# A perceiver layer on one core: the first 512 context rows by seven half-size products, their keys turned through DRAM

## The chip, the cores and the metric

The kernel runs on one core of a Trainium2 chip. A core has TensorE (PE, matrix products, with PEld its weight loads), VectorE (DVE), ScalarE (ACT), GpSimd (POOL) and SyncE (SP, which here only issues DMAs). Each engine works through its own queue in order. The metric is the device time of one execution, in microseconds (us), as the median of three executions.

## The reference

One layer with three parts on 256 tokens `x` of width 512: cross attention, a state-space block, and a mixture of 32 experts. Only the first part matters here:

```
xn = layernorm(x)                              # 256 x 512
q, k0, v0 = xn @ wq, xn @ wk, xn @ wv          # 16 heads, 4 key heads, head size 128; q and k0 are
                                               # normed per head and rotated by position (rope)
k1, v1 = ctx @ wk_ctx, ctx @ wv_ctx            # ctx: 4096 x 512; each product is 4096 x 512; keys normed
out = softmax(q [k0 k1]^T) [v0 v1]             # the 256 own keys are masked causally
x = x + out @ wo
```

Everything is float32.

## The kernel before

The context's 4096 rows are cut into eight steps of 512 rows (`NC = 8`, `CK = 512`). The attention goes through stage s = 0, the 256 own tokens, and then s = 1 to 8, one context step each. While stage s runs its scores (L668) and values (L693), the keys and values of the next context step are computed beside it, so step 0 is computed before the attention, in an opening stage, together with the own keys, queries and values.

**The two ways of a context step.** A step multiplies a 512 x 512 block of `ctx` with `[wk_ctx | wv_ctx]`, 512 x 1024. Steps 1 to 7 use `fast_steps`, a recursive scheme of seven products (a Strassen form: sums and differences of the quarters of both operands, seven products in place of eight), on two levels. Step 0 is done plainly by `context_pieces(0)`: for each of four tiles of 128 rows, `key_piece` and `value_piece` make a 128 x 512 result from four matmuls each (L225, helper `project`), ACT copies it out of PSUM, `key_rms` squares the keys on ACT and makes a factor on POOL, and `key_transpose` (L296 to L302) turns the four heads of a tile by four PE transposes and an ACT copy. In the profile a float32 matmul with 512 columns shows as two records, so a piece is eight records.

**Turning without PE.** `turn_heads` (L264 to L273) turns a 128 x 512 tile otherwise: DVE transposes 32 x 32 blocks into a tile `tr`, SP issues four stores of `tr` to a DRAM block (`kd` or `qd`), and then one load of the turned block into `kT` or `qT`, which waits until the stores have landed. These five DMAs are pinned in program order on SP's queue. `tr` has two buffers. Own keys and the queries of heads 0 to 11 are turned so (eight blocks of 128 x 512: k0, k1, q00, q01, q10, q11, q20, q21; q with the group of four heads first, then the token tile). The queries of the last group are turned by PE (`selfT`, L575).

**One own block** (`self_block`): four matmuls into one of two PSUM banks of `ps_mm`; ACT copies the bank to `raw` (tag `kraw`, two buffers) and squares it; DVE makes the rope in four instructions (L541 to L544, `norm_rope`) into `o`, one of five rooms; POOL makes the norm (L200) and multiplies `o` by it (L545); then `turn_heads`.

**Order.** A planner puts the instructions of each engine in one fixed order before the kernel runs, by program order and by when it reckons inputs and buffers to be free. `tc.issue_after(ins)` queues what a block issues on the engine of `ins` behind `ins`; `tc.keep_in_program_order` pins an instruction behind all earlier ones of its engine. The list at L603 to L618 writes the opening stage out by hand: context values, own keys, the last context key tile, queries, own values, and the preparation of the weights for `fast_steps` (`weights_of`, `one`, `two`).

**Weight sums.** `weight_sums` (POOL, L338 to L340) makes the three 256 x 512 combinations T1, T2, T4 of the weights' quarters; `last_sum` (L387 to L390) makes T3 in place (`b12 = b22 - b12`, DVE) and the second-level sums of the value weights (`second_sums("wv")`, POOL, four instructions of L379 to L382) during stage 0, behind a mask of the attention.

**Loads.** SP loads, in this order: context tile 0 of step 0, `wk_ctx` quarters 0 and 1, then 2 and 3 in one, `x`, context tile 1, tiles 2 and 3, `wv_ctx`, then `wk`, `wq` group 0, `wv`, `wq` groups 1 to 3, and context steps 1 and 2 into the two buffers of `ctxp`.

Of the kernel before, what the change touches and what calls it, by code (L numbers as in the profile page):

```python
# [19 lines left out]
P = 128  # L20
# [55 lines left out]
def perceiver_layer(ctx: ExitStack, tc: tile.TileContext, a: dict, out: bass.AP):  # L76
# [25 lines left out]
    load_wkc(2, 2)  # L102
    nc.sync.dma_start(x_sb, a["x"].rearrange("(t p) d -> p t d", p=P))
    load_ctx0(1, 1)
    load_ctx0(2, 2)
    nc.sync.dma_start(wvc, a["wv_ctx"].rearrange("(k p) n -> p k n", p=P))
# [34 lines left out]
    def layer(ctx, bounded):  # L141
# [71 lines left out]
        def turn_xn(t, tp, halves=False):  # L213
# [4 lines left out]
            for copy, ks in (((V.tensor_copy, slice(0, KD // 2)), (S.copy, slice(KD // 2, KD))) if halves else  # L218
                             ((V.tensor_copy, slice(0, KD)),)):
                copy(xT[:, ks, t * P:(t + 1) * P], tp.rearrange("p (k n) -> p k n", k=KD)[:, ks])  # L220
# [22 lines left out]
        ctx_tiles = {0: ctx0}  # L243

        def load_ctx(c):
            ct = ctxp.tile([P, CK // P, KD, P], FP, tag="ctx", name="ctx")
            nc.sync.dma_start(ct, a["ctxT"][c])
            ctx_tiles[c] = ct

        wk = wpiece(a["wk"], "wk")  # L250
        wq = [wpiece(a["wq"][:, 0:512], "wq0")]
        wv = wpiece(a["wv"], "wv")
        wq += [wpiece(a["wq"][:, j * 512:(j + 1) * 512], f"wq{j}") for j in range(1, 4)]
        load_ctx(1)
# [55 lines left out]
        def context_pieces(c):  # L310

            ct = ctx_tiles.pop(c)
            v, r, raws, key_transpose, _ = context_tiles(c)

            def key_piece(i):
                ps = ps_mm.tile([P, 512], FP, tag="mm", name="ps_k")
                project(ps, lambda k: ct[:, i, k, :], lambda k: wkc[:, k, :])
                raws[i] = raw = krp.tile([P, NKV, HD], FP, tag="kraw" if i == 1 else "kn", name="kraw")
                S.copy(raw, ps.rearrange("p (h d) -> p h d", d=HD))
                key_rms(raw, r[:, i, :])  # L320

            def value_piece(i):
                ps = ps_mm.tile([P, 512], FP, tag="mm", name="ps_v")
                project(ps, lambda k: ct[:, i, k, :], lambda k: wvc[:, k, :])
                S.copy(v[:, i, :], ps)

            return [[lambda i=i, f=f: f(i) for i in range(CK // P)] for f in (key_piece, value_piece, key_transpose)]

# [55 lines left out]
        def last_sum():  # L387

            V.tensor_tensor(b12, b22, b12, ALU.subtract)
            each(second_sums("wv"))  # L390
# [3 lines left out]
        def fast_steps(c, behind=None):  # L394
# [19 lines left out]
            def sums():  # L414
# [4 lines left out]
                left("P6", S2)  # L419
                G.tensor_tensor(S3, a11, a21, ALU.subtract)  # L420
# [110 lines left out]
        heads_done = []  # L531

        def norm_rope(ps, t, tb):
# [10 lines left out]
            V.tensor_tensor(o, o, u, ALU.add)  # L544
# [7 lines left out]
        ctx_k, ctx_v, ctx_t = context_pieces(0)  # L552
        for t in range(NT):
            normed = layernorm(t)
        for i in range(3):
            ctx_k[i]()
        for t in range(NT):
            turn_xn(t, ps_sc.tile([P, 512], FP, tag="sc", name="lnT"))
        rope_table(tab_k, kw_bc)
        rope_table(tab_q, qw_bc)  # L560
# [27 lines left out]
        turns = ctx_t[0:3]  # L588

        def last_key():  # L590
            ctx_k[3]()
            return ctx_t[3]
# [8 lines left out]

        weights_of = lambda: next(placed)
        one, two = lambda: behind_head("t"), lambda: behind_head("t4", 2)  # L603
        for f in (ctx_v[0], lambda: k_of(0), lambda: k_of(1), last_key, *q[0], ctx_v[1], weights_of, lambda: self_value(0),
                  q[1][0], one, q[1][1], one, lambda: self_value(1), weights_of, q[2][0], one, q[2][1], one, ctx_v[2],
                  q[3][0], two, q[3][1], two, ctx_v[3]):
            turn = f()
            if f not in (weights_of, one, two):
                turns.append(turn)
            while len(turns) > 2:  # L610
# [23 lines left out]
        pin(nc.sync.dma_start(by_head, a["by_head"].partition_broadcast(P)))  # L634
# [1180 lines left out]
```

## Time and profile before

| | us |
|---|---|
| median of 3 executions | 963.77 (963.64 to 963.96) |
| the profiled execution | 961.0 |
| its span (first to last instruction) | 959.2 |
| PE busy in the span | 939.9 |
| DVE, ACT, POOL busy | 571.4, 383.0, 429.3 |
| opening stage, from the first matmul to the last plain piece | 5.45 to 78.9 |
| stage 0 of the attention | 79.3 to 101.1 |

The span is one profiled execution, and the profile's times count from its start. A group line gives the source line, engine, operation, output and inputs, shape, number, the time busy and the mean of one; a timeline line gives start, time, the same names, and in brackets how long the engine sat idle before it and what ended that. PE's busy time is modelled, since matmuls are pipelined, so the distances between starts are the better measure of what one costs.

### The profile page before, as it was taken

To read this page: it belongs to the slowest core of one execution; us is meant where nothing else is said; L and a number is where in the kernel's file an instruction comes from. 1 tells how busy PE (TensorE), PEld (TensorE's weight loads), DVE (VectorE), ACT (ScalarE), POOL (GpSimd) and SP (SyncE) were. 2 spreads that over 40 slices of the span, in tenths; PEclk is the share of its full clock that TensorE was granted. 3 is DMA by queue.
4 is the path that set the end of the run, shared out by engine and by line. 5 is a ranking of instruction groups with operands and counts; after the bars stand their busy time and mean duration, and the time that the engine had idled before them with its cause. 6 is when DMAs were issued, how large, how long until landed. Compare 5 with 4: busy or idle time off the path is not lost.

```text
span 959.2 us, 10117 instructions
## 1 busy us (share of the span) xinstructions
PE 939.9 (98%) x3025; PEld 508.0 (53%) x3025; DVE 571.4 (60%) x1205; ACT 383.0 (40%) x872; POOL 429.3 (45%) x487
## 2 busy tenths in 40 slices
PE   7999999999999999999999999999999999999996
PEld 3444555555555555555555555544465655555442
DVE  4458766566566656665756656658497666632223
ACT  3646444344344444343443444443253742122221
POOL 3559956345444644634724723300013234545542
PEclk9999999999999999999999999999999999999999
DMA  9732053053034015104205203360046453899983
GB/s 328 241 78 47 0 176 87 1 154 89 1 86 141 15 35 174 35 14 152 77 1 153 67 1 88 81 228 0 0 157 209 165 196 122 327 328 366 362 322 109
DMA packets 130803, 124.93 MB, mean 130 GB/s; under 512 B 80017, under 2 KB 99250, under 8 KB 125490
## 3 DMA queue, kind: packets, MB, share of 16 engines
q1 hardware_dynamic: 119216, 77.96, 26.9%
q0 software_dynamic: 7904, 40.90, 11.7%
q10 hardware_dynamic: 3618, 5.33, 1.5%
q8 instruction: 26, 0.43, 0.2%
q14 instruction: 39, 0.32, 0.1%
HBM read 88.76 MB, written 35.41 MB: 129 GB/s over the span
## 4 chain that ended last, share of the span: by engine, by line
PE 95%; issue 1%; POOL 1%; DVE 1%; DMA 1%; ACT 0%; SPq 0%; POOLq 0%; DVEq 0%
PE oT L693 24%; PE scT L668 24%; PE ps_kv L459 15%; PE ps_egu L225 5%; PE ps_self L225 4%; PE ps_v L225 2%; PE ps_o L892 2%; PE ps_xbc L225 2%; PE ps_k L225 2%; PE ps_ye L1616 2%; PE ps_out L1089 1%; PE ps_z L225 1%; PE ps_sgu L225 1%; PE ps_ye L1619 1%; PE xgTp L1495 1%
## 5 line engine op out<-in xcount | busy, mean ns | idle before, releaser
L684 DVE TENSOR_TENSOR lacc<-lacc,prT 128x512 f32<-128x512 f32 x256 | 200.6, 785 | 197.3 <-ACT prT L674 196.2
L674 ACT ACTIVATE prT<-scT,bq,rk 128x512 f32<-128x512 f32 x256 | 198.4, 775 | 280.4 <-PE scT L668 269.5
L668 PE MATMUL scT<-qT,kT 128*128 128x512 f32 x536 | 273.5, 592 | 0.0
L693 PE MATMUL oT<-prT,v 128*128 128x512 f32 x528 | 269.4, 592 | 0.1
L693 PEld LDWEIGHTS oT<-prT,v 128*128 128x128 f32 x528 | 100.1, 190 | 125.8 <-issue 117.9
L668 PEld LDWEIGHTS scT<-qT,kT 128*128 128x128 f32 x536 | 101.2, 190 | 41.0 <-issue 30.6
L459 PE MATMUL ps_kv<-fast,ctx 128*128 128x256 f32 x350 | 99.6, 379 | 0.0
L459 PEld LDWEIGHTS ps_kv<-fast,ctx 128*128 128x128 f32 x350 | 66.4, 190 | 48.3 <-issue 39.9
L410 POOL TENSOR_TENSOR ctx<-ctx 128x128 f32<-128x128 f32 x21 | 11.4, 542 | 98.7 <-PE ps_kv L459 98.7
L200 POOL TENSOR_TENSOR rk<-pv,mhalf 128x4 f32<-128x4 f32 x32 | 37.4, 1180 | 28.0 <-DVE pv L199 28.0
L262 ACT ACTIVATE xn<-kraw 128x128 f32<-128x128 f32 x112 | 33.5, 301 | 39.4 <-POOL kraw L434 22.1
L459 PE MATMUL ps_kv<-wkv,ctx 128*128 128x256 f32 x168 | 48.9, 379 | 0.0
L444 POOL TENSOR_TENSOR v<-fast,v 128x768 f32<-128x768 f32 x21 | 40.9, 1960 | 16.2 <-DVE fast L488 15.6
L459 PEld LDWEIGHTS ps_kv<-wkv,ctx 128*128 128x128 f32 x168 | 31.8, 190 | 28.4 <-issue 25.0
L699 DVE TENSOR_TENSOR oacc<-oT,oacc 128x512 f32<-128x512 f32 x64 | 43.6, 682 | 0.0
L1599 DVE TENSOR_TENSOR hid<-si,ps_egu 128x128 f32<-128x128 f32 x18 | 5.2, 287 | 47.5 <-ACT si L1597 47.5
L459 PE MATMUL ps_kv<-fast,fast 128*128 128x256 f32 x112 | 33.3, 379 | 0.0
L459 PEld LDWEIGHTS ps_kv<-fast,fast 128*128 128x128 f32 x112 | 21.3, 190 | 17.8 <-issue 12.0
L268 DVE STREAM_TRANSPOSE tr<-kraw 128x512 f32<-128x512 f32 x28 | 18.3, 690 | 19.6 <-POOL kraw L433 19.6
L892 PE MATMUL ps_o<-wo,qT 128*128 128x512 f32 x64 | 28.8, 592 | 0.0
L1290 POOL DMA_INDIRECT xg_sb<-xg,place x16 | 15.1, 947 | 29.1 <-PE xgTp L1495 26.7
L225 PE MATMUL ps_self<-wq,xT 128*128 128x512 f32 x64 | 28.1, 592 | 0.0
(439 smaller groups left out, 1412.8 us busy)
## 6 DMA issues: line engine op xcount, KB each, us to landing
xg<-xn SPq DMA_DIRECT2D x6, 2560.0 KB, 9.4
ctx<-in_ctxT_dram SPq DMA_DIRECT2D x7, 1024.0 KB, 5.0
kd<-tr SPq DMA_DIRECT2D x112, 64.0 KB, 2.2
kT<-kd SPq DMA_DIRECT2D x28, 256.0 KB, 3.0
ye<-y_sb ACTq DMA_DIRECT2D x19, 256.0 KB, 8.3
wq<-in_wq_dram SPq DMA_DIRECT2D x4, 1024.0 KB, 14.4
wo<-in_wo_dram SPq DMA_DIRECT2D x4, 1024.0 KB, 7.9
w_in<-in_W_inT_dram SPq DMA_DIRECT2D x4, 1024.0 KB, 8.7
```

The costliest lines, as they stand in the source:

```text
L200: return G.tensor_tensor(dst, v[:, :n], mhalf[:, :n], ALU.pow)
L225: TE.matmul(ps, lhs(k), rhs_of(k), start=(k == 0), stop=(k == KD - 1))
L262: S.activation(sq[:, h, :], raw[:, h, :], AF.Square, accum_out=ss[:, h:h + 1])
L444: G.tensor_tensor(to[:, 1:4], q, base[:, 1:4], ALU.add)
L459: TE.matmul(b[n], sets[name][i], y, start=start, stop=True, skip_group_check=True)
L668: scored.append(TE.matmul(sc, kT[:, g, i * P:(i + 1) * P], qT[:, t, heads4(g), :].rearrange("p h q -> p (h q)"), start=True, stop=True).ins)
L674: S.activation(pr, sc, AF.Exp, bias=shift, scale=SCALE if r is None else r[:, i, g:g + 1])
L684: V.tensor_tensor(la, la, pr, ALU.add)
L693: TE.matmul(outs[g, t], v[:, i, g * HD:(g + 1) * HD], pr, start=(n == 0), stop=last)
L699: V.tensor_tensor(ov, outs.pop((g, t)), ov, ALU.add)
L892: TE.matmul(m["ps_o", t], aT[:, t, h, :], wo[j][:, h % 4, :], start=(h == 0), stop=(h == NH - 1))
L1616: TE.matmul(ps[i], h[:, i, :], wd[i], start=True, stop=False)
```

## The change

Step 0 is computed by seven products on one level (`first_step`). With A the four quarters of the context block (a11, a12, a21, a22: two row tiles by two halves of the inner dimension) and B those of `[wk_ctx | wv_ctx]` (b11, b21 the key weights, b12, b22 the value weights):

```
S1 = a21 + a22;  S2 = S1 - a11;  S3 = a11 - a21;  S4 = a12 - S2      (POOL)
T1 = b12 - b11;  T2 = b22 - T1;  T3 = b22 - b12;  T4 = b21 - T2
P1 = a11 b11   P2 = a12 b21   P3 = S4 b22   P4 = a22 T4   P5 = S1 T1   P6 = S2 T2   P7 = S3 T3
keys of tiles 0, 1 = P1 + P2             values of tiles 0, 1 = P1 + P6 + P5 + P3
keys of tiles 2, 3 = P1 + P6 + P7 + P4   values of tiles 2, 3 = P1 + P6 + P7 + P5
```

Each product is two row tiles (j = 0, 1) of two matmuls with 512 columns. P2 is added to P1, and P3 to P5, in the same PSUM bank, after the first has been read. The keys are turned by `turn_heads` (DVE, SP, DRAM) instead of PE. P1 and P2 open the kernel; the other products stand between the own blocks. The diff, cut to what the prediction speaks of:

```diff
     load_ctx0(0, 1)
     load_wkc(0, 1)
     load_wkc(1, 1)
-    load_wkc(2, 2)
+    load_ctx0(1, 1)
     nc.sync.dma_start(x_sb, a["x"].rearrange("(t p) d -> p t d", p=P))
-    load_ctx0(1, 1)
-    load_ctx0(2, 2)
-    nc.sync.dma_start(wvc, a["wv_ctx"].rearrange("(k p) n -> p k n", p=P))
+    load_wkc(2, 1)
+    load_wkc(3, 1)
...
             ct = ctxp.tile([P, CK // P, KD, P], FP, tag="ctx", name="ctx")
-            nc.sync.dma_start(ct, a["ctxT"][c])
+            with tc.issue_after(settled[0]) if c == 2 else nullcontext():
+                nc.sync.dma_start(ct, a["ctxT"][c])
...
         wk = wpiece(a["wk"], "wk")
+        nc.sync.dma_start(wvc, a["wv_ctx"].rearrange("(k p) n -> p k n", p=P))
+        load_ctx0(2, 2)
         wq = [wpiece(a["wq"][:, 0:512], "wq0")]
...
+        first_sums = ctxp.tile([P, CK // P, KD, P], FP, tag="ctx", name="first_sums")
         load_ctx(1)
...
-        def context_pieces(c):
...
-        def last_sum():
-            V.tensor_tensor(b12, b22, b12, ALU.subtract)
-            each(second_sums("wv"))
+        def first_step(sums):
+            ct = ctx_tiles.pop(0)
+            v, r, raws, key_transpose, key_blocks = context_tiles(0)
+            T1, T2, T4 = sums
+            S1, S2, S3, S4 = carve(first_sums, *[OP] * 4)
+            def bank(held=False):
+                p, tag = (ps_mm, "mm") if held or not bounded else (ps_sc, "sc")
+                return p.tile([P, 512], FP, tag=tag, name="ps_first")
+            def product(ps, lhs, rhs, j, start=True):
+                for k in range(2):
+                    TE.matmul(ps, lhs[:, j, k, :], rhs[:, k, :], start=(start and k == 0), stop=(k == 1),
+                              skip_group_check=True)
+                return ps
+            def key(i):
+                raws[i] = krp.tile([P, NKV, HD], FP, tag="kn", name="kraw")
+                return raws[i]
+            def key_done(i):
+                key_rms(raws[i], r[:, i, :])
+                (key_blocks if bounded else key_transpose)(i)
+            def p1(j):
+                x[j] = product(bank(True), a11, b11, j)
+                S.copy(v[:, j, :], x[j])
+            def p2(j):
+                product(x[j], a12, b21, j, False)
+                S.copy(flat(key(j)), x.pop(j))
+            def p6(j):
+                V.tensor_tensor(v[:, j, :], product(bank(), S2, T2, j), v[:, j, :], ALU.add)
+            def p7(j):
+                V.tensor_tensor(v[:, 2 + j, :], product(bank(), S3, b12, j), v[:, j, :], ALU.add)
+            def p4(j):
+                V.tensor_tensor(flat(key(2 + j)), product(bank(), a22, T4, j), v[:, 2 + j, :], ALU.add)
+                key_done(2 + j)
+            def p5(j):
+                z[j] = product(bank(True), S1, T1, j)
+                V.tensor_tensor(v[:, 2 + j, :], z[j], v[:, 2 + j, :], ALU.add)
+            def p3(j):
+                product(z[j], S4, b22, j, False)
+                V.tensor_tensor(v[:, j, :], z.pop(j), v[:, j, :], ALU.add)
+            def t3():
+                V.tensor_tensor(b12, b22, b12, ALU.subtract)
...
                 left("P6", S2)
+                if c == 1:
+                    each(second_sums("wv"))
                 G.tensor_tensor(S3, a11, a21, ALU.subtract)
...
-        ctx_k, ctx_v, ctx_t = context_pieces(0)
+        p1, p2, p3, p4, p5, p6, p7, sums12, sums34, t3, key_done = first_step(sums)
         for t in range(NT):
             normed = layernorm(t)
-        for i in range(3):
-            ctx_k[i]()
+        for f in (p1, p2) if bounded else ():
+            for j in range(2):
+                f(j)
...
         for t in range(NT):
-            turn_xn(t, ps_sc.tile([P, 512], FP, tag="sc", name="lnT"))
-        rope_table(tab_k, kw_bc)
-        rope_table(tab_q, qw_bc)
+            turned = turn_xn(t, ps_sc.tile([P, 512], FP, tag="sc", name="lnT"))
+        with tc.issue_after(turned.ins):
+            for j in range(2) if bounded else ():
+                key_done(j)
+            rope_table(tab_k, kw_bc)
+            rope_table(tab_q, qw_bc)
...
-        for f in (ctx_v[0], lambda: k_of(0), lambda: k_of(1), last_key, *q[0], ctx_v[1], weights_of, lambda: self_value(0),
-                  q[1][0], one, q[1][1], one, lambda: self_value(1), weights_of, q[2][0], one, q[2][1], one, ctx_v[2],
-                  q[3][0], two, q[3][1], two, ctx_v[3]):
+        for f in (*of_heads[0:1], one_two, *of_heads[1:2], three_four, *q[0], weights_of,
+                  lambda: self_value(0), last_first, q[1][0], one, *both(p6), q[1][1], one, lambda: self_value(1), weights_of,
+                  *both(p7),
+                  q[2][0], one, q[2][1], one, *both(p4), q[3][0], two, q[3][1], two, *both(p5), *both(p3)):
...
-            while len(turns) > 2:
+            while len(turns) > 3:
...
-        pin(nc.sync.dma_start(by_head, a["by_head"].partition_broadcast(P)))
+        settled.append(pin(nc.sync.dma_start(by_head, a["by_head"].partition_broadcast(P))).ins)
...
-                    if s == 0 and n == 8:
-                        with tc.issue_after(masked[-1]):
-                            last_sum()
```

`one_two` and `three_four` issue S1, S2 and S3, S4 on POOL behind the norm of the block before them; `last_first` issues T3 on DVE behind the last rope. `bounded` is the branch that runs here. The two reductions of the norm weights in `bounded_attention` are queued behind `turned` as well.

## The prediction, put on record before the change was run

> **What bounds the kernel now.** I read the page's busy times and its chain of waits first, then PE's timeline over the opening stage, then the queues of SP, DVE and ACT in it.
>
> ```profile
> PE 939.9 (98%) x3025; PEld 508.0 (53%) x3025; DVE 571.4 (60%) x1205; ACT 383.0 (40%) x872; POOL 429.3 (45%) x487
> PE 95%; issue 1%; POOL 1%; DVE 1%; DMA 1%; ACT 0%; SPq 0%; POOLq 0%; DVEq 0%
> ```
>
> PE is busy 98% of the span and makes 95% of the chain that ended last. A stage gets shorter only if PE gets less to do in it, and it loses whatever PE then waits. So I count PE's work in the opening stage:
>
> ```profile
> 5.45 12.42 PE L225 MATMUL ps_k<-wkv,ctx 128*128 128x512 f32 x24 [5.45 <-DMA wkv<-in_wk_ctx_dram]
> 17.70 1.04 PE L216 MATMUL lnT<-ident,xn 128*128 128x128 f32 x8
> 18.58 3.60 PE L225 MATMUL ps_v<-wkv,ctx 128*128 128x512 f32 x8
> 22.01 0.60 PE L299 MATMUL kTp<-ident,kraw 128*128 128x128 f32 x4
> 22.45 1.02 PE L225 MATMUL ps_self<-wk,xT 128*128 128x512 f32 x2
> ...
> 75.47 3.60 PE L225 MATMUL ps_v<-wkv,ctx 128*128 128x512 f32 x8
> 78.91 0.60 PE L575 MATMUL selfT<-ident,lacc 128*128 128x128 f32 x4
> ```
>
> From start to start, a piece of eight records takes 78.91 - 75.47 = 3.44 us: 0.43 a record, 0.86 a float32 matmul. Four key transposes take 22.45 - 22.01 = 0.44; the other three sets take 0.50, 0.50 and 0.49. The stage holds 20 pieces (16 + 16 + 48 matmuls): 20 x 3.434 = 68.7, with 1.93 of key transposes and 0.88 of `lnT` 71.5. From 5.45 that ends at 76.9, against 78.9 in the trace. The missing 2 us are all at the start:
>
> ```profile
> 8.14 0.34 PEld L225 LDWEIGHTS ps_k<-wkv,ctx 128*128 128x128 f32 x1 [0.52 <-DMA wkv<-in_wk_ctx_dram]
> 8.99 0.32 PEld L225 LDWEIGHTS ps_k<-wkv,ctx 128*128 128x128 f32 x1 [0.52 <-issue]
> 9.55 0.19 PEld L225 LDWEIGHTS ps_k<-wkv,ctx 128*128 128x128 f32 x1 [0.24 <-issue]
> 9.98 0.19 PEld L225 LDWEIGHTS ps_k<-wkv,ctx 128*128 128x128 f32 x1 [0.24 <-issue]
> ```
>
> Records stand 0.86 apart until 9, then 0.43. After that PE never waits until the attention.
>
> **What the change takes from PE.** Eight products become seven: 32 matmuls become 28, 4 x 0.858 = 3.43 us. The 16 key transposes go: 1.93. Together **5.36 us**, all on the path.
>
> **The opening.** P1 is eight records, as the first piece was: it ends at 10.85 (the ninth record's load stood at 10.84). Its four loads are the first MiB of the queue, and in the old order tile 1 landed with 2.0 MiB at 9.9 (issued 3.2, landed 6.7 later). P2 needs 2.0 MiB, so 9.9: in time. P2 adds to the bank that ACT must first copy out. The first copy came behind a load of ACT's tables:
>
> ```profile
> 11.09 1.28 ACT L319 ACT_TABLE_LOAD   x1 [11.09 <-DMA tables<-in_tables_dram]
> 12.38 0.59 ACT L319 COPY kraw<-ps_k 128x512 f32<-128x512 f32 x1
> ```
>
> The first piece ended at 10.85, so I take this start as PE's release. P1's first tile ends at 9.0; 0.2 + 1.28 + 0.59 + 0.1 later P2 may start, at 11.2: **0.35 lost**. If it is the DMA of `tables` (issued 4.7, landed 6.9 later) it is 13.5, 2.6 lost. P2 ends at 14.65, `lnT` at 15.5 (`xn` was there at 12.7 in the old order, and `x` now lies 0.25 MiB earlier). Before, a value piece of 3.4 us lay over DVE's copies of `xT` (1.27 for two). Now the first own block follows at once: first half turned at 15.1, copy 0.64 and two hand-overs, start at 16.05: **0.5 lost**. Putting the rope tables and reductions behind these copies costs nothing: the rope waits for block k0 at about 20, and they take 2.3 us. `wk` moves from 4.5 MiB down the queue (landed 19.5) to 3.0; between tile 2-3 (2.5 MiB, 11.6) and `wv_ctx` (3.5 MiB, 16.9) that is 14.3, at worst 16.9, 0.9 late. `wq` group 0 stays at 5.5 MiB, landed 22.2, and is wanted at 22.9. After it each MiB lands 2.65 us later and is wanted later still.
>
> So PE's stage runs to 14.65 + 0.88 + 0.5 + 12 own blocks (41.2) + five products (17.2) = 74.4 instead of 78.9: **4.5 us** gained.
>
> **The rest, beside PE.**
> - ACT loses eight copies (12 become 4): 4.7 us less.
> - DVE gets ten additions from PSUM (0.68 each by the row of L699) and four transposes of 0.7; T3 (1.48) moves here from stage 0. That is 11 us more on some 35 busy out of 61 between 17.9 and 79.3: room, if its queue does not stand still. It stands in front of PE at P5 to P3 only, where a bank must be read first; four own matmuls lie between.
> - POOL gets S1 to S4, four of 1.26 to 1.75 (rows of L417 to L422), on 36 busy in the same 61. S2 is wanted by P6 at 36, and the weight sums that start with `wv_ctx` (0.5 MiB later, about 18) end at 25.5. The sums "wv" of four instructions stood on POOL behind `left("P6")` at 102.9 already, so their new place changes nothing.
> - SP gets 20 DMAs. A block took it 4.4 us (stores 40.22, next stores 44.59), later 3.9; twelve instead of eight from 37 on end near 85. q21 is wanted near 87, keys 2 and 3 near 99. `load_ctx(2)` now comes behind that; step 2 is first read at 136 on POOL, one load takes 5.0: hidden with 40 us to spare.
> - Stage 0 loses T3 from DVE and gets up to two transposes: its 0.8 us of gaps (21.8 against 20.6 + 0.44 of work) may go or stay. Bounds: 0.8 gained, 0.5 lost; I take nothing.
>
> **The unknown: `tr` has two buffers.** Keys 0 and 1 take both at about 17, and their stores queue behind all loads:
>
> ```profile
> 21.38 3.18 SPq L247 DMA_DIRECT2D ctx<-in_ctxT_dram  x2
> 32.38 3.47 SPq L271 DMA_DIRECT2D qd<-tr  x4
> 39.73 0.38 SPq L273 DMA_DIRECT2D kT<-qd  x1
> 40.22 2.19 SPq L271 DMA_DIRECT2D qd<-tr  x4
> 44.16 0.38 SPq L273 DMA_DIRECT2D kT<-qd  x1
> ```
>
> Step 2's load landed at 38.2 and the first stores at 39.6, 1.4 behind it. Now the last load ahead is step 1's, 35.6, so key 0's stores land near **37.0**, and only then can DVE turn k0. What stands behind that in DVE's fixed queue waits too. If the rope of k1 stands behind, its `raw` stays taken, ACT cannot copy q01, PE's bank stays taken and q10 waits. If it stands ahead, only blocks with free buffers are delayed. The trace speaks for the second, weakly:
>
> ```profile
> 65.99 0.69 DVE L541 TENSOR_TENSOR lacc<-raw,oacc 128x512 f32<-128x512 f32 x1 [0.20 <-ACT raw L536]
> ...
> 74.31 0.70 DVE L268 STREAM_TRANSPOSE tr<-lacc 128x512 f32<-128x512 f32 x1
> ```
>
> The transpose of q20, whose input POOL had finished at 67.6, stands a block late, behind q21's rope (65.99) and within q30's, though q10's buffer was free from 61.3 on, when its load was issued: the planner reckons `tr` busy longer than it is. But with both buffers fresh, k0's transpose at 31.64 stands ahead of k1's rope at 32.27. Bounds: 0 to 7.1 us; I take 0, by the row with `tr` in use, which is k0's case after.
>
> **Two rules of the Trainium skill.** "TensorE: Matmul & The Clock Gate", HAM oscillation, says that a gap over some 3.4 us halves PE's clock for the next 3.4. The rows above show a slow start like that, and no gap later. By that rule a wait of 7 us would cost an estimated 1.7 us more; the two gaps of 0.35 and 0.5 cost nothing more. "DMA: Bandwidth & Descriptors", Specifications, wants runs of 512 B or more, and these stores write runs of 128 B, which speaks against turning through DRAM. The trace has such a block at 3.9 to 4.4 us of SP's time, off PE's path, in place of 0.5 of PE; the sum stays the same by either, unless rival 3 holds.
>
> **Rivals.**
> 1. *The opening waits longer* (0.20): ACT's tables come with their DMA, 2.25 more, or `wk` at its worst, 0.9 more. Gain 1.0 to 3.5; **961.6**. Against it: 11.09 lies ahead of 11.6.
> 2. *DVE stands in front of k0's transpose* (0.24), slower: q10, due at 33.2, starts 3.3 after the stores land (hand-over 0.2, transpose 0.7, three rope instructions 1.4, hand-over 0.2, ACT's copy 0.6, hand-over 0.2): 40.3, so 7.1 lost and 2.6 net: **966.4**. It turns a gain into a loss when the stores land later than 34.4 (33.2 + 4.5 - 3.3).
> 3. *The end of the stage waits* (0.10): keys 2 and 3 or the last ropes come late behind SP's twelve blocks, 1 to 6 us: about **962.8**.
>
> That the products are not spared cannot be: the matmuls are counted in the code.
>
> **The numbers.** Forecast (0.46): 4.5 off the span of 959.2 gives 954.7; the profiled execution's own time lies 1.8 above its span, so 956.5 against 961.0. The median shown is 2.8 above that execution, and I take the same 4.5 off it: 963.77 - 4.5 = **959.3**; own range 957.8 (the opening's 0.85 and most of stage 0's gaps gone) to 960.4. A measurement tells 0.2%, 1.9 us, from no change. Faster by more: 0.46, 0.12 of the first rival, 0.04 of the third: 0.62. Same: 0.08 + 0.06 + 0.04 = 0.18. Slower: 0.18 of the second, 0.02 of the third: 0.20. The range runs from 957.8 to the second rival's 966.8; some 0.15 lies outside.
>
> **What would show it.** Right: no `kTp`, 28 matmuls of step 0, `selfT` near 74.4 with PE gapless from 16; P2 near 11.2; DVE idle near 37 before a transpose while PE runs on. Wrong: PE idle between 33 and 40 with ACT waiting for DVE; P2 at 13 or later; PE waiting before P3 or at the start of stage 1.

## The result and the profile after

The changed kernel takes **971.41 us** (967.62 to 973.85, 11 executions), the kernel before 963.96 beside it: ratio **1.0068** [1.0051, 1.0085], slower. (The ratio is estimated from all the executions of both; the two medians alone would give 1.0077.) The forecast was 959.3 with a range up to 966.8. Wrong in sign, and outside the range.

The profiled execution took 972.06 (span 970.3), 11.1 more span than the one before. The busy times are not the reason. PE has the 24 records less that were counted (eight for four matmuls, sixteen transposes), 3025 to 3001. Its busy time falls by only 1.0 in place of the 5.36 of the forecast; P6's slow records, below, are 1.7 of the difference:

```profile
PE 938.9 (97%) x3001; PEld 505.5 (52%) x3001; DVE 586.5 (60%) x1219; ACT 378.8 (39%) x864; POOL 433.8 (45%) x491
PE 90%; DMA 3%; DVE 2%; POOL 2%; issue 1%; ACT 1%; SPq 1%; POOLq 0%; DVEq 0%; ACTq 0%
```

In the second line, the chain that ended last, PE fell from 95% to 90%, and DMA, DVE and POOL stand in it with 2 to 3% each. The change did not make PE's work longer, it made PE wait. Where, is read from the starts of the stages:

| us from the span's start | before | after |
|---|---|---|
| first scores of stage 0 (`scT`) | 79.34 | 78.92 |
| first product of step 1, in stage 1 (`ps_kv`) | 101.14 | 110.05 |
| `ps_pick`, behind the attention and the state-space block | 814.72 | 823.29 |
| from there to `ps_ye`, in the experts | 18.6 | 21.6 |

The opening stage ends 0.4 earlier (4.5 were forecast), stage 0 takes 31.1 in place of 21.8, and the 8.9 so lost are carried to the end almost unchanged (8.6 at `ps_pick`). The last row is no effect of the change: over all profiles of this study that stretch takes 18.6 us (13 times) or 20.9 to 21.9 (7 times), with and without each part of the change. Where the record names the chip, it goes by the chip: 20.9 to 21.9 in all six profiles of one chip, 18.6 in all twelve of the three others. For the two profiles above no chip is named. So 3.0 of the 11.1 are most likely the chip's; the medians, of runs side by side, differ by 7.5.

PE's queue shows the places. Columns: start, duration, engine, line, operation, number of records, and in brackets the idle time before and what ended it.

```profile
4.68 9.78 PE L383 MATMUL ps_first<-wkv,ctx 128*128 128x512 f32 x16 [4.68 <-DMA wkv<-in_wk_ctx_dram]
14.29 1.04 PE L215 MATMUL lnT<-ident,xn 128*128 128x128 f32 x8
15.73 4.53 PE L225 MATMUL ps_self<-wk,xT 128*128 128x512 f32 x10 [0.39 <-ACT sq L266]
...
38.80 5.40 PE L383 MATMUL ps_first<-oacc,first_sums 128*128 128x512 f32 x8 [2.23 <-POOL first_sums L425]
...
75.38 3.70 PE L383 MATMUL ps_first<-wkv,first_sums 128*128 128x512 f32 x8
78.92 1.02 PE L732 MATMUL scT<-qT,kT 128*128 128x512 f32 x2
82.37 0.66 PE L630 MATMUL selfT<-ident,lacc 128*128 128x128 f32 x4 [2.43 <-POOL lacc L592]
...
85.53 1.13 PE L757 MATMUL oT<-lacc,v 128*128 128x512 f32 x2 [0.79 <-DVE lacc L741]
...
89.84 1.13 PE L732 MATMUL scT<-qT,kT 128*128 128x512 f32 x2 [1.47 <-DMA qT<-qd]
...
94.87 1.12 PE L732 MATMUL scT<-qT,kT 128*128 128x512 f32 x2 [1.33 <-DMA qT<-qd]
...
99.34 1.12 PE L732 MATMUL scT<-qT,kT 128*128 128x512 f32 x2 [2.48 <-DMA qT<-qd]
```

There are two kinds. In the opening stage P6 waits 2.23 for S2 (`first_sums` from POOL), and its eight records then take 5.40 where the eight of P3, at 75.38, take 3.70: the granted clock, the share of full speed at which PE is run, is 0.67 over 38.8 to 44.0. In stage 0 five waits add up to 8.5: 2.43 for the rope of q31, 0.79 for a mask, and 5.3 for the queries q11, q20 and q21 on their way through DRAM. Those are the change's losses; the two largest are followed here, the rope of q31 further down.

**P6's chain**, in the chain of work up to 45 us (start, duration, engine, tile, line):

```profile
19.90 1.99 DVE oacc L575
22.08 2.39 DVE oacc L575
...
31.39 1.39 POOL r L199
32.84 1.35 POOL lacc L592
34.19 1.74 POOL first_sums L424
35.94 1.41 POOL first_sums L428
37.34 1.42 POOL first_sums L425
38.80 5.40 PE ps_first L383 x8
```

S1 (L424) was to be queued behind k0's norm on POOL. In the planner's order k1's norm stands ahead of it too (the rows of L199 and L592 at 31.39 and 32.84; k0's are at 28.48 and 29.93), which takes 2.8 us, and S3 (L428) stands before S2 (L425), another 1.4. Both norms are late because the rope tables (L575) are: they now stand behind the copies of `xT`, thus beside POOL's weight sums, and two of these DVE instructions take seven and nine times what the third takes:

```profile
19.83 2.06 DVE L575 TENSOR_TENSOR oacc<-tables,w_bc 128x128 f32<-128x128 f32 x1
...
22.01 2.47 DVE L575 TENSOR_TENSOR oacc<-tables,w_bc 128x128 f32<-128x128 f32 x1
...
24.60 0.28 DVE L575 TENSOR_TENSOR oacc<-tables,w_bc 128x128 f32<-128x128 f32 x1
```

**The queries' chain** starts on DVE. When each of the last three blocks is turned, by the starts of `STREAM_TRANSPOSE`:

| us | q11 | q20 | q21 | first scores |
|---|---|---|---|---|
| before | 65.09 | 74.31 | 81.80 | 79.34 |
| after | 81.05 | 87.67 | 90.41 | 78.92 |
| `four_tr` (below) | 74.20 | 80.93 | 87.37 | 84.07 |
| `four_tr_p6_p7_later` (below) | 69.17 | 75.76 | 82.34 | 79.05 |

After the turn a block still needs its stores and its load: q21's transpose at 90.41 ends in the scores at 99.34. So the queries are turned 9 to 16 us later than before, and the DVE queue, not the transfer, decides when. Block q01 in the changed kernel, in the queues of POOL, SP and DVE:

```profile
45.31 1.04 POOL L592 TENSOR_TENSOR lacc<-lacc,r 128x512 f32<-128x512 f32 x1
...
55.67 0.38 SPq L277 DMA_DIRECT2D kT<-qd  x1
...
70.56 0.70 DVE L272 STREAM_TRANSPOSE tr<-lacc 128x512 f32<-128x512 f32 x1
```

POOL had its input ready at 46.35. Its `tr` buffer held k1 before, whose load was issued at 55.67, behind its landed stores. DVE stood idle for 3.36 us before 58.59, and the transpose came at 70.56. A real lack of buffers explains only the start: key tiles 0 and 1 held both until 35.8 and 40.3, but k0 and k1 were turned at 44.29 and 51.44.

### The profile page after: what moved, and what is told of

Its sections match the earlier page's. It is cut to its first block, busy times and chain, and to the rows that moved or that the text cites. A ratio compares the mean times of both kernels' runs of the same rounds, so it can differ in the third digit from the quotient of the medians.

```text
span 970.3 us, 10129 instructions
## 1 busy us (share of the span) xinstructions
PE 938.9 (97%) x3001; PEld 505.5 (52%) x3001; DVE 586.5 (60%) x1219; ACT 378.8 (39%) x864; POOL 433.8 (45%) x491
## 4 chain that ended last, share of the span: by engine, by line
PE 90%; DMA 3%; DVE 2%; POOL 2%; issue 1%; ACT 1%; SPq 1%; POOLq 0%; DVEq 0%; ACTq 0%
PE oT L757 23%; PE scT L732 23%; PE ps_kv L506 15%; PE ps_egu L225 5%; PE ps_first L383 3%; PE ps_o L951 2%; PE ps_xbc L225 2%; PE ps_self L225 2%; PE ps_ye L1675 2%; PE ps_out L1148 1%; PE ps_z L225 1%; PE ps_sgu L225 1%; PE ps_ye L1678 1%; PE xgTp L1554 1%; DMA ye<-y_sb 1%
## 5 line engine op out<-in xcount | busy, mean ns | idle before, releaser
L748 DVE TENSOR_TENSOR lacc<-lacc,prT 128x512 f32<-128x512 f32 x256 | 197.9, 774 | 199.2 <-ACT prT L738 197.9
L199 POOL TENSOR_TENSOR rk<-pv,mhalf 128x4 f32<-128x4 f32 x32 | 37.4, 1182 | 27.1 <-DVE pv L198 27.1
L272 DVE STREAM_TRANSPOSE tr<-kraw 128x512 f32<-128x512 f32 x32 | 21.1, 692 | 19.9 <-POOL kraw L480 19.9
L453 POOL TENSOR_TENSOR ctx<-fast 128x128 f32<-128x128 f32 x28 | 20.4, 727 | 19.7 <-PE ps_kv L506 19.2
```

The lines of the kernel that those rows point to most:

```text
L199: return G.tensor_tensor(dst, v[:, :n], mhalf[:, :n], ALU.pow)
L748: V.tensor_tensor(la, la, pr, ALU.add)
```

## The experiments

The kernel before took 959.9 to 965.2 on the chips used, so each kernel is told by its ratio to the kernel before on its own chip, with the 95% interval. In the texts on record T is the theory held at that point (T, then T2, T3, T4 as each was replaced) and R1, R2 are its rivals: R1 that SP's queue and DRAM cannot carry twelve blocks, R2 that the rope tables' new place costs PE time.

### One part undone, one part alone

**`keys_by_pe`** turns step 0's four key tiles on PE again:

```diff
-                (key_blocks if bounded else key_transpose)(i)
+                return lambda: key_transpose(i)
...
-            for j in range(2) if bounded else ():
-                key_done(j)
+            turns = [key_done(j) for j in range(2)]
...
```

> The changed kernel, but step 0's keys are turned by PE (four transposes and an ACT copy a tile) as before the change; the seven products stay. Theory T (DVE's fixed order: keys 0 and 1 stand first in the two `tr` buffers, so the own blocks are turned late and stage 0 waits for them): stage 0's 8.5 us of PE waits fall to the 0.8 of the kernel before (7.7 less), PE gets 1.93 of transposes back, P6's wait of about 4 stays: 971.4 - 5.8 = 965.6. Rival R1 (SP and the DMA queues cannot carry twelve blocks): the same 965.6, since four blocks go; the DVE order in the next runs has to tell it from T. Rival R2 (rope tables behind the copies, POOL's chain and P6's late S2 hold everything up): stage 0 still waits, 971 to 973.

Measured **1.0122** [1.0076, 1.0168]. Not faster than the change; T, that keys 0 and 1 in `tr` hold the queries up, fell in this form. Two of the three late queries do come in time here (q11 and q20 are turned at 69.29 and 75.47), but PE waits as long for q21 alone, 5.18:

```profile
97.71 2.08 PE L728 MATMUL scT<-qT,kT 128*128 128x512 f32 x2 [5.18 <-DMA qT<-qd]
```

```profile
87.33 0.97 DVE L737 TENSOR_TENSOR lacc<-lacc,upper 128x512 f32<-128x512 f32 x1 [0.94 <-ACT lacc L734]
88.22 0.70 DVE L272 STREAM_TRANSPOSE tr<-lacc 128x512 f32<-128x512 f32 x1
```

The second fence is DVE's queue of the same kernel: the transpose of q21 stands behind a mask of stage 0 that had to wait for ACT.

**`p6_later`** moves P6 behind q11 in the written-out list:

```diff
-                  lambda: self_value(0), last_first, q[1][0], one, *both(p6), q[1][1], one, lambda: self_value(1), weights_of,
+                  lambda: self_value(0), last_first, q[1][0], one, q[1][1], one, *both(p6), lambda: self_value(1), weights_of,
```

> The changed kernel, but P6 stands one own block later (behind q11), so S2 (ready at 38.8) is there when PE wants it. T: P6's wait of 2.2 and the 1.8 of half clock go, but the transposes stand as late as before and stage 0 waits for them: between 967.4 (all 4.0 gained, where DVE's queue moves up with PE) and 971.4 (none, where SP's blocks set the end). R1: 971, SP's twelve blocks set the end. R2: at least the 4.0, and stage 0's waits shrink with it: 963 to 967.

Measured **1.0049** [1.0032, 1.0066]. P6 does not wait any more, and the scores start at **74.52**. But the first product of stage 1 starts at 110.57, later than after's 110.05: in this execution, what the opening stage gained, stage 0 waited away. 3.4 us of that is a wait for a mask that took 5.98 on DVE, which `four_tr_products_spread` takes up. The profiled execution (971.05) is one of the slowest of twelve (median 968.23), so in the others a part of the gain may be left; the two intervals overlap.

**`keys_by_pe_p6_later`** has both edits.

> Both edits together. T: the two causes add up: 965.6 - 4.0 = 961.6, below the kernel before (964.0) by about 2.4, since 4 matmuls (3.43) are spared less 0.85 of opening gaps. R1: the same. R2: rope tables still stand behind the copies and the ropes are late: 965 or more.

Measured **1.0067** [1.0046, 1.0088]; one wait of 4.97 for a query is left, and the granted clock is 0.57 in the 3.4 us behind it.

**`dram_alone`** is the kernel before with nothing but the keys' way through DRAM (`key_blocks` in the place of `key_transpose`; eight plain pieces, the old order of loads).

> The kernel before with only one part of the change: its eight plain pieces stay, but the four key tiles are turned through DRAM instead of by PE. PE does 1.93 less. T: key tiles 0 and 1 take both `tr` buffers first, queries q11 to q21 are turned at or after the start of stage 0, the scores wait: 963 to 968, no gain from 1.93 less work. If turning through DRAM cost nothing (my prediction's step): 962.0. R2 (the loss comes from the products' chain on POOL and the rope tables, not from the turning): 962.0 too.

Measured **1.0116** [1.0082, 1.0150], 975.19: that it does not gain was expected, the size (963 to 968) was not. Its waits (who, for what; total, number, longest):

```profile
PE scT L668 <- DMA qT<-qd: 5.6, 5, 2.4
...
PE oT L693 <- DVE lacc L677: 3.6, 1, 3.6
```

No half-size product is in this kernel, and the queries are as late as in the change. Four more blocks through `tr` alone cost as much as the change lost, by the medians more. With `keys_by_pe` (1.0122, DVE loaded by the products' additions) it speaks for either half of the change being enough to make DVE's queue late.

### The order of DVE's queue, or the transfer?

**`turns_ahead`** queues the rope of block n+3 behind the transpose of block n, and the masks of stage 0 behind q21's transpose (`own_at` collects the transposes):

```diff
...
-            V.tensor_tensor(o, raw, cs, ALU.mult)
...
+            with tc.issue_after(own_at[-3]) if len(own_at) >= 3 else nullcontext():
+                V.tensor_tensor(o, raw, cs, ALU.mult)
...
-                    masked.append(V.tensor_tensor(p3, p3, upper.unsqueeze(1).to_broadcast([P, REP, P]), ALU.mult).ins)
+                    with tc.issue_after(own_at[-1]):
+                        masked.append(V.tensor_tensor(p3, p3, upper.unsqueeze(1).to_broadcast([P, REP, P]), ALU.mult).ins)
```

> The changed kernel with only DVE's order edited: the rope of the third own block after a block stands behind that block's transpose, and stage 0's masks stand behind q21's. So all eight own transposes come ahead of the attention. After the first four runs the theory is T2: not keys 0 and 1 in `tr` delay the queries (they came as late without them), but the place of the last own transposes in DVE's fixed queue, behind three or more masks of stage 0. T2: stage 0's waits (8.5 us between 78.9 and 110.05 where the kernel before had 0.8) fall by 7 to 7.7, P6's wait and half clock (4.0) stay: stage 1 starts near 102.5, 963.5 to 965. R1 (SP and the queues cannot carry the blocks in time): the queries land as late as before, 970 or more. R2 (late ropes and POOL's chain): DVE or POOL waits take their place, 968 or more.

Measured **1.0080** [1.0063, 1.0097]. **`turns_ahead_p6_later`** adds the later P6:

> The same, and P6 one own block later. T2: both losses gone, stage 1 starts near 98.5 and the time is 959.5 to 961, the 4.5 us that the prediction counted minus up to 1. R1: 969 or more. R2: PE waits at P5, P3 or selfT, since ropes and norms are late: 964 or more.

Measured **1.0053** [1.0038, 1.0068]. T2, that the order of DVE's queue alone was to blame, was right on the place and wrong on the price. The wait for the queries goes from 5.3 to 0.4 and comes back as a wait for the last group's rope (here `turns_ahead_p6_later`; the other's rows are 5.5 and 0.4):

```profile
PE selfT L635 <- POOL lacc L595: 5.3, 2, 5.1
...
PE scT L737 <- DMA qT<-qd: 0.4, 1, 0.4
```

The 5.1 are for q30's rope, which now starts at 80.33, right behind q11's transpose at 79.71; that one stands late in DVE's order too, since its buffer was free from 69.10, when q01's load was issued. That the queries come almost in time with the same twelve blocks on SP's queue speaks against R1, but weakly, since PE's 5.1 us at `selfT` give them that much longer.

**`keys_by_pe_turns_ahead_p6_later`** (lag 2 in place of 3):

> Seven products, keys turned by PE, P6 later, and own transposes ahead (two blocks behind instead of three, since no keys are in `tr`). T2: 1.93 of PE transposes more than the run with keys through DRAM: 961.5 to 963. R1: four blocks fewer on SP, so the same 961.5 to 963, and clearly below the run with keys through DRAM. R2: 964 or more.

Measured **1.0016** [1.0005, 1.0028]: fewer blocks, DVE's order forced, `selfT` still waits 2.92; T2 had forecast a time below the kernel before. **`dram_alone_turns_ahead`**:

> The kernel before with its key tiles turned through DRAM (no seven products), and the own transposes ahead. T2: the 12 us that the plain version of this lost go, and the 1.93 of PE transposes are gained: 961.5 to 963. R1: twelve blocks on SP still come too late: 966 to 975.

Measured **1.0088** [1.0071, 1.0104], with waits of 5.94 and 1.88 before `selfT`, where T2 had forecast a gain.

**`four_tr`** takes away what the planner reckons with: two of the three rooms of `u`, a tile of the rope, serve as two more spaces for `tr`, for the twelve blocks of the opening stage (`u` keeps one). The list, the products and the transfers are those of the change.

```diff
-            tr = krp.tile([P, REP * HD], FP, tag="tr", name="tr")
+            tr = (rooms_tr[n % 4].rearrange("p h d -> p (h d)") if n < 12 and n % 4 < 2 else
+                  krp.tile([P, REP * HD], FP, tag="tr", name="tr"))
...
-        take_ro, take_ru = ring([room[i] for i in (0, 1, 4, 5, 7)]), ring([room[i] for i in (2, 6, 3)])
+        take_ro, take_ru = ring([room[i] for i in (0, 1, 4, 5, 7)]), ring([room[2]])
+        rooms_tr += [room[6], room[3]]
```

> The changed kernel with only the spaces for `tr` edited: four instead of two in the opening. T3: the two `tr` buffers, as the planner reckons them, set the place of the transposes; P6's wait and the selfT wait stay. The changed kernel stands at 1.0068 of before, and with P6 later four spaces were worth 0.0026: 1.004, between 1.003 and 1.005. R1 (SP's twelve blocks in themselves): 1.0068 as the changed kernel.

Measured **1.0029** [1.0018, 1.0040] against the change's 1.0068. Its waits of PE up to 120 us have no `scT` line at all:

```profile
PE ps_first L388 <- POOL first_sums L430: 2.9, 1, 2.9
PE selfT L636 <- POOL lacc L598: 1.6, 1, 1.6
...
PE oT L763 <- DVE lacc L747: 1.1, 2, 0.7
```

This settles the queries: the same bytes in the same order on the same queue, and none is late. By the table above q21 is turned 3.3 us behind the first scores in place of 11.5. A part of that, 5.15, is that the scores start later here; but in absolute time too q11, q20 and q21 are turned 6.9, 6.7 and 3.0 earlier, and `four_tr_p6_p7_later`, whose scores start at 79.05 as the change's do at 78.92, turns q21 at 82.34 and never waits for a query. So **R1 is refuted**.

The edit also takes two of `u`'s three rooms, and no run has that alone. The planner's order can be read without running a kernel: with `u` cut to one room and `tr` left at two, DVE's queue has the change's order, instruction for instruction. So it is the two more spaces for `tr` that move the transposes. The two buffers were the cause in the change, through the planner: it reckons a buffer busy for longer than it is (the rows of q01 above), puts other DVE work in front of the transpose, and that order is then fixed. At no time did DVE stand and wait for a `tr` buffer. Why q21 is late in `keys_by_pe`, with no more blocks in `tr` than the kernel before, was not tried with four spaces. What is left, P6's wait, now costs 2.93 and a half clock (its eight records take 6.74).

### What is left, wait by wait

The next kernels keep the four spaces (or the keys on PE) and move one wait each. Pn names a product's entry in the list.

**`four_tr_p6_later`:**

> The changed kernel with P6 one own block later and four spaces for `tr` instead of two during the opening (two rooms taken from the ring of the rope's second factor `u`, which keeps one). Theory T3: the planner puts the own transposes late because it reckons the two `tr` buffers taken by the blocks before; with four it puts q20's ahead of P3's last addition and q21's behind the first mask, as the kernel before had it. The queries then land in time, and of stage 0's waits only selfT's 2.4 stays: 1.001 to 1.003 of before, against 1.0049 of the run with P6 later alone. R1 (SP's twelve blocks take too long in themselves): no gain, 1.004 to 1.006.

Measured **1.0023** [1.0014, 1.0032]. P6 is served, and P7, one own value tile behind, waits for P6's addition on DVE instead:

```profile
51.87 3.44 PE L388 MATMUL ps_first<-wkv,first_sums 128*128 128x512 f32 x4 [2.65 <-DVE v L411]
```

**`four_tr_p6_later_products_first`** puts P4, P5 and P3 ahead of q30 and q31 to get DVE's additions out of the way of q31's rope:

> The same, and P5 and P3 (four pieces, 6.9 us of PE) stand ahead of q30 and q31, so that their six additions no longer stand among the last ropes in DVE's queue. T3 with its second part (the last ropes wait behind additions that wait for PE, so selfT of q31 is late): selfT's wait shrinks if the rope of q31 is what is late, and 0.997 to 1.001 of before. If only the distance from q31's matmuls to its selfT counts (7.4 us in the kernel before, for ACT, DVE and POOL in turn), it waits as long or longer here, since no PE work stands behind q31 but scores: 1.002 to 1.005.

Measured **1.0088** [1.0075, 1.0101]: worse, and above both ranges. With no product between q31 and `selfT`, its rope has less time; `selfT` waits 2.50 and 1.34, with a clock of 0.53 in the 3.4 us behind the first, and one more product waits 1.04 for an addition on DVE. **`keys_by_pe_p6_later_products_first`** and the same with **`_rope_free`** (the rope tables no longer queued behind the copies of `xT`):

```diff
-            rope_table(tab_k, kw_bc)
-            rope_table(tab_q, qw_bc)
+        rope_table(tab_k, kw_bc)
+        rope_table(tab_q, qw_bc)
```

> Seven products, keys turned by PE, P6 later, P5 and P3 ahead of q30 and q31, two `tr` buffers. The planner now puts selfT behind the first values, and q21's transpose behind three masks and a copy. T3: selfT does not wait; q21's load does, by 1 to 4 us: 1.001 to 1.005 of before, against 1.0067 without the edit.

> The same, and the rope tables no longer queued behind the copies of `xT` (they stand ahead of them, beside the opening's matmuls, and ahead of POOL's weight sums). T3: nothing waits for the tables once P6 is later, so no change against the run without this edit, within 0.0015. R2 (late ropes hold everything up): 0.002 or more faster than it.

Measured **1.0036** [1.0011, 1.0062] and **1.0022** [1.0013, 1.0031]. The two intervals overlap, the first product of stage 1 moves by 0.1: here the rope tables' place costs nothing that can be told.

**`four_tr_p6_p7_later`** moves P7 as well, to behind q20:

> Four spaces for `tr`, P6 behind q11 and P7 behind q20. In the run with four spaces and P6 later, PE waited 2.65 us at P7 for P6's additions, which stand in DVE's queue behind q11's rope, and 1.58 at selfT. T3: P7's 2.65 go: 1.0023 - 0.0028 = 0.9995 of before, 0.9985 to 1.0005. If another wait takes their place (P4's or P5's additions), 1.001 to 1.002.

Measured **0.9993** [0.9985, 1.0002], as expected: the change brought back to the time of the kernel before. `selfT` still waits 0.64 and 1.72.

**`four_tr_products_spread`** puts the second own value tile between q31 and P5, so that q31's rope gets 3.4 us more:

> The same, and the second own value tile moved from behind P6 to between q31 and P5, so that selfT of q31 has 3.4 us more PE work ahead of it. T3: selfT's 1.58 go too: 0.9975 to 0.999 of before, the first version below it. That leaves the opening's 0.4 and 0.3 and small waits in stage 0. If selfT waits again (its chain through ACT, DVE and POOL took 7.4 us in the kernel before): 0.999 to 1.0005.

Measured **1.0183** [1.0170, 1.0196], the worst of all, where 0.9975 to 0.999 was expected. One wait does it:

```profile
98.08 2.07 PE L762 MATMUL oT<-lacc,v 128*128 128x512 f32 x2 [14.96 <-DVE lacc L746]
```

It waits for one DVE instruction, a mask, which takes 0.7 to 1.8 us in the kernel before:

```profile
82.21 15.82 DVE L746 TENSOR_TENSOR lacc<-lacc,upper 128x512 f32<-128x512 f32 x1 [0.94 <-ACT lacc L743]
```

It ended at 98.03. POOL, which runs the sums of step 1 back to back meanwhile, had its first break from 97.48 to 97.56:

```profile
96.97 0.51 POOL L459 TENSOR_TENSOR ctx<-ctx,fast 128x128 f32<-128x128 f32 x1
...
97.56 0.79 POOL L461 TENSOR_TENSOR ctx<-fast,ctx 128x128 f32<-128x128 f32 x1
```

That made T4: a DVE instruction with two inputs in SBUF may not get in until POOL stops. **`four_tr_products_spread_rope_free`** has the mask at 15.80 as well:

> The same, and the rope tables not queued behind the copies of `xT`. T3: nothing waits for them once P6 is later: within 0.001 of the run without this edit. R2: 0.002 faster or more.

Five of its six executions took 973.5 to 974.8 and one 956.9, so the wait is presumably not there each time (one execution has a profile), and no ratio is given. It taught nothing on the rope tables.

**`products_spread_pool_gap`** tests T4. Two one-column copies on POOL read the first two masked tiles, and step 1's sums are queued behind the second, so POOL pauses until the masks are through:

```diff
...
+                    if len(masked) < 3:
+                        gaps.append(G.tensor_copy(small.tile([P, 1], FP, tag="gap", name="gap", bufs=1), pr[:, 0:1]).ins)
...
-                    extra = fast_steps(s, heads_done[-1] if s == 1 else None)
+                    extra = fast_steps(s, gaps[-1] if s == 1 else None)
```

> The run with the products spread lost 15 us in one place: DVE's first mask (0.69 elsewhere) took 15.82 us, from 82.21 to 98.03, while POOL went through sums from 81.44 to 97.48 without a break, and it ended in POOL's first break. Theory T4: a DVE tensor_tensor with both inputs in SBUF waits for POOL's, and while POOL's sums follow without a break it may not be let in at all. Here POOL gets two one-column copies that read the first two masked tiles, and step 1's sums stand behind them, so POOL must wait for DVE there; nothing else is changed. T4: the 15 us go: 1.0183 - 0.0160 = 1.002 of before or less (0.998 to 1.002). Rival: the mask waits for something that the profile doesn't show (ACT, a transfer): 1.016 to 1.020 as before the edit.

Measured **1.0004** [0.9985, 1.0022], from 1.0183, by an edit that adds work:

```profile
82.57 1.14 DVE L746 TENSOR_TENSOR lacc<-lacc,upper 128x512 f32<-128x512 f32 x1 [0.94 <-ACT lacc L743]
```

The same mask, 15.82 before, takes 1.14: a break in POOL's run takes the wait away, as T4 says. It is not needed every time, though. In the kernel before POOL runs from 82.74 to 99.95 without a break as well, and six masks get in meanwhile, in 0.76 to 1.76 us each. Here is one of them in DVE's queue, between the two rows of POOL beside it:

```profile
87.94 1.28 POOL L381 TENSOR_TENSOR fast<-wkv,fast 128x512 f32<-128x512 f32 x1
...
88.55 1.23 DVE L677 TENSOR_TENSOR prT<-prT,upper 128x512 f32<-128x512 f32 x1 [0.89 <-ACT prT L674]
...
89.18 0.91 POOL L408 TENSOR_TENSOR ctx<-ctx 128x128 f32<-128x128 f32 x1
```

What decides whether a mask is let in between two sums or kept out by all of them stays open. What is left is P7's wait of 3.10 and the half clock behind it. **`products_spread_rope_free_pool_gap`** also frees the rope tables:

> The same, and the rope tables not queued behind the copies of `xT`. Without the edit, five of six executions took 973.5 to 974.8 and one 956.92. T4: all lie near the one, 956 to 959, or 0.996 to 0.999 of before: the first version below it. Rival: as without the edit, near 974.

Measured **0.9963** [0.9944, 0.9982], 961.96 against 965.16: faster than both kernels. Rows of PE's queue:

```profile
50.23 1.98 PE L388 MATMUL ps_first<-wkv,first_sums 128*128 128x512 f32 x4 [1.99 <-DVE v L411]
...
77.58 2.74 PE L737 MATMUL scT<-qT,kT 128*128 128x512 f32 x6
...
99.42 0.59 PE L511 MATMUL ps_kv<-wkv,ctx 128*128 128x256 f32 x2
```

Stage 0 is back to 21.8 us, as in the kernel before, and starts 1.8 earlier. Freeing the rope tables was worth 0.0041 here and 3.2 us at the start of stage 1, though only about 2 us of k0's chain moved (its transpose from 30.79 to 28.73): P7's wait fell from 3.10 to 1.99, and the clock stayed up. So R2 is right in this kernel. In the earlier pair the same edit moved nothing: k0's transpose stood at 29.84 without it and at 29.73 with it, since with the tables gone two instructions of k0's rope itself took 2.94 and 2.62 beside POOL's weight sums.

## Why the prediction was wrong, point by point

- **PE's side held.** 5.36 off PE and the end of the opening stage 4.5 earlier were right as a sum: `p6_later`, in which P6 is not held up, starts its scores at 74.52; the forecast gives 74.4 + 0.44 for a set of turns that stands before them, less 0.5 for the opening (k0 at 15.54 there in place of 16.05), 74.3.
- **The opening** was cheaper than forecast: `lnT` starts at 14.29 (forecast 14.65), k0 at 15.73 (16.05). ACT's table load came with PE's first result, as assumed, not with the DMA of `tables`; rival 1 did not happen (by its own terms its gain would have been 1.35 to 3.6, not 1.0 to 3.5):

```profile
8.83 1.28 ACT L399 ACT_TABLE_LOAD   x1 [8.83 <-PE ps_first L383]
```

- **"S2 is wanted by P6 at 36, weight sums end 25.5" was costed at nothing; it cost 2.23 of waiting and 1.7 of slow clock.** The step counted POOL's work and not what stands before it: S1 and S2 are issued behind k0's norm, and in the planner's order behind k1's too, which need the ropes, which need the rope tables; S3 stands between them. S2 was done at 38.76.
- **"Putting the rope tables and reductions behind these copies costs nothing"** failed with it. The 2.3 us were the durations in their old place; beside POOL's sums two rows of 0.28 took 2.06 and 2.47, and k0's rope, forecast at about 20, started at 26.2. In the last kernel this place is worth 3.2 us at the start of stage 1; in the pair before it was worth nothing.
- **"`tr` has two buffers … Bounds: 0 to 7.1 us; I take 0" failed, and this is the largest term:** 5.3 us of PE's waits. The bounds were for q10 in the opening stage (rival 2), where DVE never waited for a `tr` buffer. The price came in stage 0, since each transpose had been planned too late. The row that showed it was in the prediction: q20's transpose at 74.31, a block late though its buffer was free, with the right reading ("the planner reckons `tr` busy longer than it is"). It was used to choose between two orders, not as a price: in the kernel before q21's transpose at 81.80 was already behind the start of the scores, and in `dram_alone` four more blocks alone pushed the queries further.
- **SP's "end near 85"** was not met: the stores of q21 were issued at 92.28. The queue had room (`four_tr` passes the same blocks through it), its input was late.
- **"It stands in front of PE at P5 to P3 only"** failed: `selfT` waited 2.43 for q31's rope, whose first and last steps stood behind P3's second addition. An addition in DVE's queue delays what is behind it, whether or not PE waits for the addition:

```profile
79.12 0.69 DVE L421 TENSOR_TENSOR v<-ps_first,v 128x512 f32<-128x512 f32 x1 [0.41 <-PE ps_first L383]
79.72 0.68 DVE L588 TENSOR_TENSOR lacc<-raw,oacc 128x512 f32<-128x512 f32 x1
80.44 0.69 DVE L591 TENSOR_TENSOR lacc<-lacc 128x512 f32<-128x512 f32 x1
```

- **Rival 3**, "the end of the stage waits", named the right place with 0.10 and 1 to 6 us. It was 8.5, and its cause was not SP. That it would decide the sign was not seen, because it was weighed as SP's rival and priced without DVE's order.
- **The clock rule** of the Trainium skill ("TensorE: Matmul & The Clock Gate", HAM oscillation: a gap over some 3.4 us) was used to say that short gaps cost nothing more. The trace disagrees: a wait of 2.23 (3.06 between its weight loads) was followed by a mean granted clock of 0.67 over 38.8 to 44.0.

What stays open: whether and why `dram_alone` and `keys_by_pe` are slower than the whole change (their intervals touch or overlap the change's). The profile of `dram_alone` shows late queries and a wait of 3.62 for a mask, but what puts them later than in the change was not tried by itself. Nor is it settled how large the last kernel's gain is: the interval allows 1.7 to 5.4 us, the medians differ by 3.2, and 1.7 are seen at the start of stage 1.

## What to carry to other kernels

Where a planner fixes each engine's order beforehand, a scarce buffer costs time without any instruction ever waiting for it: look for a row that stands later than its inputs and its real buffers require, ask what more such rows would cost at the next stage that reads them, and try it with more buffers before blaming the transfer. Follow each new consumer's input back through every queue it passes (here S2, k0's norm, the rope tables), with the durations of the new neighbours, not of the old place. And taking one wait away shows the next: the gain counts only at the end of the last stage that waits.

## What the runs showed of the hardware

**The clock falls after waits well under 3 us.** Behind PE waits of 2.65, 2.92, 2.93, 3.10 and more the mean granted clock of the next 3.4 us was 0.50 to 0.59, each time. Below that it went both ways: it fell after 2.23, 2.37 and 2.50, and not after 1.99, 2.04, 2.39, two of 2.43, and 2.48. These are gaps between PE's records, whose ends are modelled. Between weight loads they are up to 0.8 longer (3.48 at the 2.65), but there too the clock fell after 3.06, 3.16, 3.20 and 3.30, and not after 3.21, 3.26 and 3.31. The two last kernels side by side, over 50 to 56 us (PE, PEld, DVE, ACT and POOL busy with their records, then the granted clock, DMA's share and GB/s); the wait of the first, 3.10, ends at 52.29, that of the second, 1.99, at 50.23:

```profile
50.00:56.00 6.00, 3.71 (x5) 1.70 (x6) 6.00 (x11) 0.00 (x0) 5.13 (x6) 0.72 0.56 103
```

```profile
50.00:56.00 6.00, 5.76 (x14) 2.66 (x15) 6.00 (x11) 0.31 (x1) 5.11 (x5) 1.00 0.64 136
```

The same page (Part 1, on the clock gate) says that the window by which idleness is judged runs freely; waits of one length that go both ways agree with that.

**DVE can be shut out by POOL for far longer than one instruction.** The Trainium skill ("SBUF — State Buffer", SBUF: two separate sides) says that the ports which DVE and GpSimd share are locked for a whole instruction, and that a DVE instruction with two SBUF inputs contends with GpSimd's reads. The rope tables agree with one instruction's lock (0.28 became 2.06 and 2.47 beside sums of about 2.4). The long masks do not: 15.82 and 15.80 passed while POOL ran one sum of 0.5 to 1.3 after another, and 5.98 in `p6_later`, each ending 0.5 to 0.6 behind the end of POOL's run. With a break made in the run it was 1.14. But it does not happen each time that POOL runs on: six masks in the kernel before took 0.76 to 1.76 beside sums that touch one another.
